# A four-layer graph network on one core: the test for the general path at the last head's end, layer 2's weights, degrees and first adjacency rows ahead of the skipped loops

## The chip, the cores and the metric

The kernel runs on one core of a Trainium2 chip. The metric is the device time of one execution in microseconds. The kernel before took 4518.02 us (median of three runs, 4509.77 to 4524.34).

## The reference

The input is a matrix x of N = 2708 nodes with C = 128 features and a weighted adjacency matrix adj (2708 x 2708, a few neighbours a row and the diagonal), all in float32. Four layers follow each other, each as x = x + layer(relu(layernorm(x))).

```python
# layer 0
d = adj.sum(1); s = 1 / (sqrt(d) + 1e-8)
out = (adj * s[:, None] * s[None, :]) @ (h @ W + b)
# layer 1: 128 "heads" d of width 8
q, k, v = (h @ Wq.T).reshape(128, n, 8), ...
a = softmax(q @ k.T * 128**-0.5 + adj + adj, axis=2)   # n x n for every head
out = (a @ v).reshape(n, 1024) @ Wo.T
# layer 2
deg = adj.sum(1, keepdims=True); deg = where(deg == 0, 1, deg)
t = (adj.T @ h / deg) @ W_n.T + b_n + h @ W_c.T + b_c
out = relu(gamma * (t - mean(t)) * rsqrt(var(t) + 1e-5) + beta)
# layer 3
gate[i, j] = sigmoid(a[j] + b[i] + b1) * adj[i, j]
out = einsum('ijf,jg->ig', gate, h) @ weight + bias
```

## The kernel before, in words

Nodes lie in 22 row tiles (NT = 22) of 128 partitions, the last of 20 rows (`rows`); x stays in SBUF as `x_sb`. Columns of a 2708-wide row are cut into six pieces of at most 512 (`cols`).

Layer 1 does not form its 128 softmax matrices. For every head the exponential is replaced by a polynomial in q·k, so that a head needs only features of its keys and queries (128 of each) and moments of its values; the adjacency bias acts only where adj is not zero, and is brought in as a correction, gathered neighbour by neighbour. One part of the program, `with tc.manual_schedule()`, is an order written out by hand. Its main loop runs over the heads (`for d in range(D)`, D = 128), and inside a head over six chunks of row tiles (`for c in range(NCH)`). A head's work:

- `keys` and `with_values` on POOL: features of the keys (`fk`) and values times features (`y`, L1010, 2 instructions a head).
- `queries` on DVE: features of the queries (`fq`, L1007).
- `moments` on PE (`m_ps`, L1048), then `weighted` on DVE (`mw`, L1058).
- `turn`: transposes of `fq` on PE (L1074) and their copy on ACT (L1076).
- `evaluate`: the product with the moments on PE (`g_ps`, L1086), and on DVE the multiplication `z` (L1094) and the reduction into `o_raw` (L1100).

Four heads make a group (GRP = 4), 32 groups in all. After a group `sums` adds the values' sum on POOL (L693) and SP stores it to `o_g` (L696).

Beside the heads run two things. `first` is a generator: the search for the neighbours and their gathers, logits and values, the corrections of the softmax (DMA_INDIRECT from POOL at L825, DVE at L840, L870, L878). PACE says how many of its steps are taken for each chunk; in the kernel before it is 1.30. Once `first` is exhausted, up to three calls of `step` a chunk work on the list `beside`: 32 `normalise(g)` and 22 `project_out(t)`. At most two of them are under way at a time, and each waits three chunks (WAIT) behind its loads. After the loop over the heads a `while` loop takes what is left in `beside`: I call this the drain.

- `normalise(g)` loads a group's sums and corrections (`r_raw` L921, `r_more` L922, on SP), adds them on DVE (L930), takes the reciprocal of the last column (L932), multiplies (`r_on`, L933), and stores the result to `o_c` in DRAM with 11 to 13 DMAs from SP (L399).
- `project_out(t)` loads the row tile of all heads (`o_cr`, L499), runs 16 matmuls on PE (L505) and four additions into `x_sb` on DVE (L508).

The polynomial holds only for small logits. So behind the drain the kernel before tests the bounds (L1183 to L1223, some 20 small DVE instructions and a few PE transposes), loads the answer into registers of all engines (`values_load`, L1226 and L1227), and has a general path of three hardware loops, `For_i(0, once)` at L1229, `For_i(0, heads)` at L1241 and `For_i(0, once)` at L1295. With these inputs the counts are zero and the loops are skipped; their barriers are not.

Layer 2 follows: weights by `transposed` (load L180, PE L186, copy on DVE L189), biases by `column_of` (L172), `norm_relu` (statistics on DVE L200 and L201, the square root on ACT L203, h on DVE L206 and ACT L210, transposes L217), the inverse degree `di` (L1323 to L1325) and its spread over all partitions `diB`: for each row tile `dg` on DVE (L1329), `d_ps` on PE (L1331), a copy on ACT (L1332). Then for each of the 22 row tiles one adjacency row block `a2` is loaded (L1339, four buffers), and six matmuls add into `pg` (L1341); `ag = pg * diB` (L1346), and the rest of layer 2 and layer 3 follow.

The tile framework places everything outside the hand-written order: each engine executes its own instruction queue, and DMAs are issued mostly by SP, in the order in which they stand there. An instruction that waits for a semaphore holds what stands behind it on its engine. At a hardware loop every engine waits for the others, and the loop's block waits for the DMAs that have been issued.

Of the kernel before, what the change touches and what calls it, by code (L numbers as in the profile page):

```python
# [9 lines left out]
FP = mybir.dt.float32  # L10
AF = mybir.ActivationFunctionType
# [5 lines left out]
P = 128  # L17
# [32 lines left out]
def gnn4_kernel(  # L50
# [75 lines left out]
    few = keep.tile([P, 1], FP, name="few")  # L126

# [388 lines left out]
    with ExitStack() as ph:  # L516
# [481 lines left out]
        PACE = 1.30  # L998
# [107 lines left out]
        with tc.manual_schedule():  # L1106
# [19 lines left out]
            for d in range(D):  # L1126
# [35 lines left out]
                if (d + 2) % GRP == 0 and (d + 2) // GRP + 1 < NG:  # L1162
                    soon.append(prepare((d + 2) // GRP + 1, got))
            while beside or under_way:
                if not step(n, NG):
                    n += 1


    with ExitStack() as ph:
        gp = ph.enter_context(tc.tile_pool(name="l1g", bufs=1))  # L1170
        gw = ph.enter_context(tc.tile_pool(name="l1g_w", bufs=2))
        g_l = ph.enter_context(tc.tile_pool(name="l1g_l", bufs=1, space=PSUM))
        g_t = ph.enter_context(tc.tile_pool(name="l1g_t", bufs=1, space=PSUM))
        g_o = ph.enter_context(tc.tile_pool(name="l1g_o", bufs=1, space=PSUM))
        q_f = dram.tile([N, P, HEAD], FP, name="q_f")
        k_f = dram.tile([N, P, HEAD], FP, name="k_f")
        v_f = dram.tile([N, P, VW], FP, name="v_f")
        o_f = dram.tile([N, P, HEAD], FP, name="o_f")

        nc.vector.memset(top, 0.0)  # L1183
        p2 = gp.tile([C, 2], FP, name="p2")
        for e in range(2):
            pt = g_t.tile([P, BK], FP, name="g_tr", tag="tr")
            nc.tensor.transpose(pt[:C, :P], most2[:, e], ident)
            nc.vector.tensor_reduce(p2[:, e : e + 1], pt[:C, :P], axis=AX.X, op=ALU.max)
        nc.vector.tensor_tensor(top[:, 0:1], p2[:, 0:1], p2[:, 1:2], ALU.mult)
        nc.vector.tensor_tensor(top[:, 1:2], p2[:, 0:1], p2[:, 1:2], ALU.max)  # L1190
        nc.vector.tensor_reduce(top[:, 2:3], nval, axis=AX.XY, op=ALU.max)
        nc.vector.tensor_reduce(top[:, 3:4], nval, axis=AX.XY, op=ALU.min)
        low = gp.tile([P, 1], FP, name="low")
        nc.vector.tensor_reduce(low, least, axis=AX.X, op=ALU.min)
        nc.vector.tensor_tensor(top[:, 3:4], top[:, 3:4], low, ALU.min)
        nc.vector.tensor_scalar_mul(top[:, 3:4], top[:, 3:4], -1.0)
        nc.vector.tensor_reduce(low, below, axis=AX.X, op=ALU.max)
        nc.vector.tensor_tensor(top[:, 3:4], top[:, 3:4], low, ALU.max)
        nc.vector.tensor_tensor(top[:, 3:4], top[:, 3:4], full, ALU.max)
        pt = g_t.tile([P, BK], FP, name="g_tr", tag="tr")  # L1200
        nc.tensor.transpose(pt[:4, :P], top, ident)
        t4 = gp.tile([4, 1], FP, name="top4")
        nc.vector.tensor_reduce(t4, pt[:4, :P], axis=AX.X, op=ALU.max)
        pt = g_t.tile([P, BK], FP, name="g_tr", tag="tr")
        nc.tensor.transpose(pt[:1, :4], t4, ident[:4, :4])
        bnd = gp.tile([1, 6], FP, name="bound")
        nc.vector.tensor_copy(bnd[:, :4], pt[:1, :4])
        nc.vector.tensor_scalar(
            bnd[:, 4:5], bnd[:, 0:1], MAX_LOGIT**2, None, ALU.is_le
        )  # L1210
        nc.vector.tensor_scalar(bnd[:, 2:3], bnd[:, 2:3], float(MAX_ADJ), None, ALU.is_le)
        nc.vector.tensor_tensor(bnd[:, 4:5], bnd[:, 4:5], bnd[:, 2:3], ALU.mult)
        nc.vector.tensor_scalar(bnd[:, 1:2], bnd[:, 1:2], MOST**2, None, ALU.is_le)
        nc.vector.tensor_tensor(bnd[:, 4:5], bnd[:, 4:5], bnd[:, 1:2], ALU.mult)
        nc.vector.tensor_scalar(bnd[:, 5:6], bnd[:, 3:4], 0.0, None, ALU.is_le)
        nc.vector.tensor_scalar(ovf, bnd[:, 5:6], -1.0, 1.0, ALU.mult, ALU.add)
        pt = g_t.tile([P, BK], FP, name="g_tr", tag="tr")
        nc.tensor.matmul(pt[:, :1], ones[0:1], bnd[:, 5:6], start=True, stop=True)
        nc.vector.tensor_copy(few, pt[:, :1])
        nc.vector.tensor_tensor(bnd[:, 4:5], bnd[:, 4:5], bnd[:, 5:6], ALU.mult)  # L1220
        flag = gp.tile([1, 2], I32, name="flag")
        nc.vector.tensor_scalar(flag[:, 0:1], bnd[:, 4:5], -1.0, 1.0, ALU.mult, ALU.add)
        nc.vector.tensor_scalar(  # L1223
            flag[:, 1:2], bnd[:, 4:5], -float(C), float(C), ALU.mult, ALU.add
        )
        once = nc.values_load(flag[:, 0:1], min_val=0, max_val=1)  # L1226
        heads = nc.values_load(flag[:, 1:2], min_val=0, max_val=C)  # L1227

        with tc.For_i(0, once):  # L1229
            for r0, sz in rows:  # L1230
                for at, dst in ((0, q_f), (HEAD, k_f), (2 * HEAD, v_f)):
                    b = gw.tile([P, P, dst.shape[2]], FP, name="bounce", tag="b")
                    nc.sync.dma_start(
                        b[:, :sz], qkv_c[:, r0 : r0 + sz, at : at + dst.shape[2]]
                    )
                    nc.sync.dma_start(dst[r0 : r0 + sz].rearrange("r c h -> c r h"), b[:, :sz])

        def flat(src):
            return src.rearrange("r c h -> (r c) h")

        with tc.For_i(0, heads) as d:  # L1241
            nat = []
            for src in (q_f, k_f, v_f):
                a = gp.tile([P, NT, src.shape[2]], FP, name=f"g_nat{len(nat)}")
                f = flat(src)[bass.ds(d * N, N)]
                load_rows(nc.sync, a, f)
                nat.append(a)
            q, k, v = nat
            kT = gp.tile([HEAD, N], FP, name="g_kT")
            for t, (r0, sz) in enumerate(rows):  # L1250
                pt = g_t.tile([P, BK], FP, name="g_tr", tag="tr")
                nc.tensor.transpose(pt[:HEAD, :sz], k[:sz, t], ident[:sz, :sz])
                nc.vector.tensor_copy(kT[:, r0 : r0 + sz], pt[:HEAD, :sz])
            o = gp.tile([P, NT, HEAD], FP, name="g_o")
            for t, (r0, sz) in enumerate(rows):
                an = gw.tile([P, N], FP, name="g_adj")
                nc.sync.dma_start(an[:sz], adj[r0 : r0 + sz])
                pt = g_t.tile([P, BK], FP, name="g_tr", tag="tr")
                nc.tensor.transpose(pt[:HEAD, :sz], q[:sz, t], ident[:sz, :sz])
                qT = gw.tile([HEAD, P], FP, name="g_qT")  # L1260
                nc.vector.tensor_copy(qT[:, :sz], pt[:HEAD, :sz])
                pl = g_l.tile([P, NC, BK], FP, name="g_l")
                for c, (c0, cw) in enumerate(cols):
                    nc.tensor.matmul(
                        pl[:sz, c, :cw], qT[:, :sz], kT[:, c0 : c0 + cw], start=True, stop=True
                    )
                    nc.vector.scalar_tensor_tensor(
                        an[:sz, c0 : c0 + cw],
                        pl[:sz, c, :cw],
                        0.5,  # L1270
                        an[:sz, c0 : c0 + cw],
                        ALU.mult,
                        ALU.add,
                    )
                mx = gw.tile([P, 1], FP, name="g_mx")
                nc.vector.tensor_reduce(mx[:sz], an[:sz], axis=AX.X, op=ALU.max)
                nc.vector.tensor_scalar_mul(mx[:sz], mx[:sz], -2.0)
                nc.scalar.activation(an[:sz], an[:sz], AF.Exp, bias=mx[:sz], scale=2.0)
                po = g_o.tile([P, VW], FP, name="g_acc")
                for m, (m0, mz) in enumerate(rows):  # L1280
                    pt = g_t.tile([P, BK], FP, name="g_tr", tag="tr")
                    nc.tensor.transpose(
                        pt[:mz, :sz], an[:sz, m0 : m0 + mz], ident[:sz, :sz]
                    )
                    pT = gw.tile([P, P], FP, name="g_pT")
                    nc.vector.tensor_copy(pT[:mz, :sz], pt[:mz, :sz])
                    nc.tensor.matmul(
                        po[:sz], pT[:mz, :sz], v[:mz, m], start=m == 0, stop=m == NT - 1
                    )
# [5 lines left out]
        with tc.For_i(0, once):  # L1295
# [6 lines left out]
            for t in range(NT):  # L1302
                for _ in project_out(gw, g_t, woT, t):
                    pass
# [297 lines left out]
```

## Time and profile before

| what | value |
|---|---|
| median of 3 runs | 4518.02 us (4509.77 to 4524.34) |
| profiled execution | 4486.52 us |
| its span | 4484.7 us |
| mean granted TensorE clock | 0.837 |
| busy: PE, DVE, ACT, POOL | 72%, 82%, 25%, 57% of the span |
| last reduction of the head loop ends | 3931.8 us |
| last addition of the drain ends | 4018.42 us |
| test ends | 4023.07 us |
| third skipped loop is left | 4032.78 us |
| first pg matmul | 4047.38 us |
| pg stage ends | 4156.75 us |

Times in the profile count from the span's start, in one execution on the chip. An instruction's row gives its start, its duration, the engine, the line of the kernel, the operation, the tiles that it writes and reads, and in brackets the idle time of its engine ahead of it with the instruction that ended it. The engines are PE (matrix products; PEld is its weight load), DVE (vector), ACT (scalar), POOL (GpSimd), and SP, which issues DMAs. The granted clock is the share of full speed that PE had.

### The profile page before, as it was taken

Reading aid. Unit: us, or ns where it says so; the run is one execution under the profiler, and the core shown is the slowest. Engines: PE = TensorE matmul, PEld = TensorE weight load, DVE = VectorE, ACT = ScalarE, POOL = GpSimd, SP = SyncE. Lnnn points to the kernel's source line nnn. Section 1 sums busy time; section 2 is a strip of 40 time slices with the busy share of each in tenths; the row PEclk is TensorE's granted clock in tenths of the full one; section 3 lists DMA queues with packets and bytes.
Section 4 is the critical chain, followed back from the end, with each engine's and each line's share of the span. In section 5 each row is a group of like instructions: output and inputs, shape, how many; then the busy total and the mean of one; then the engine's idle time right before and its main releaser. Section 6 shows DMA issues by size and latency. Waiting matters only on the chain. (4 is left out here: it accounts for less than half of the span.)

```text
span 4484.7 us, 49573 instructions
## 1 busy us (share of the span) xinstructions
PE 3225.3 (72%) x17298; PEld 2876.7 (64%) x17298; DVE 3669.4 (82%) x4983; ACT 1100.2 (25%) x2497; POOL 2544.8 (57%) x2253
## 2 busy tenths in 40 slices
PE   7985778889966677677777676667676687839634
PEld 5952777788856666667666676667666677824323
DVE  5988889998868999999999998999899888831323
ACT  4255233334412222222222222222122111101201
POOL 0001766678858666677676676767576555300076
PEclk9987888999988888888888888888888788959555
DMA  4647334357702222222222222222222344447132
GB/s 186 227 154 294 86 101 110 87 126 171 164 9 84 79 75 76 89 81 83 87 76 88 77 92 78 85 86 94 86 88 88 76 97 95 107 108 262 51 100 79
DMA packets 402005, 480.24 MB, mean 107 GB/s; under 512 B 290672, under 2 KB 322098, under 8 KB 376916
## 3 DMA queue, kind: packets, MB, share of 16 engines
q1 hardware_dynamic: 370140, 308.03, 23.8%
q0 software_dynamic: 31600, 168.86, 11.2%
q8 instruction: 144, 2.36, 0.2%
q14 instruction: 121, 0.99, 0.1%
HBM read 363.13 MB, written 113.67 MB: 106 GB/s over the span
## 5 line engine op out<-in xcount | busy, mean ns | idle before, releaser
L1086 PE MATMUL g_ps<-mw,fT 128*128 128x189 f32 x5632 | 1213.3, 362 | 734.6 <-DVE mw L1058 501.9
L1086 PEld LDWEIGHTS g_ps<-mw,fT 128*128 128x128 f32 x5632 | 1032.8, 213 | 812.8 <-issue 642.2
L1010 POOL TENSOR_TENSOR y<-bk,raw 128x2079 f32<-128x2079 f32 x256 | 982.9, 3840 | 685.7 <-PE m_ps L1048 658.4
L1048 PE MATMUL m_ps<-y,fk 128*128 128x189 f32 (+1 forms) x5632 | 1108.1, 342 | 29.0 <-POOL y L1010 29.0
L1048 PEld LDWEIGHTS m_ps<-y,fk 128*128 128x128 f32 (+1 forms) x5632 | 969.2, 204 | 58.1 <-POOL y L1010 29.5
L1076 ACT COPY fT<-f_ps 128x512 f32<-128x512 f32 (+1 forms) x768 | 422.9, 551 | 1955.2 <-PE f_ps L1074 1954.3
L1094 DVE TENSOR_TENSOR z<-g_ps,bq 128x756 f32<-128x756 f32 (+1 forms) x768 | 669.1, 871 | 177.7 <-PE g_ps L1086 173.9
L1100 DVE TENSOR_REDUCE o_raw<-z 128x36 f32<-128x756 f32 (+1 forms) x768 | 672.5, 876 | 26.3
L1010 POOL TENSOR_TENSOR fk<-bk,raw 128x528 f32<-128x528 f32 (+1 forms) x512 | 526.5, 1058 | 0.0
L1074 PE MATMUL f_ps<-ident,fq 128*128 128x128 f32 x2816 | 490.8, 299 | 46.2 <-DVE fq L1007 44.6
L1074 PEld LDWEIGHTS f_ps<-ident,fq 128*128 128x128 f32 x2816 | 399.2, 157 | 83.9 <-issue 45.8
L1010 POOL TENSOR_TENSOR fk<-raw,bk 128x352 f32<-128x352 f32 (+1 forms) x512 | 337.3, 688 | 0.0
L840 DVE TENSOR_TENSOR c_z<-c_kv,c_q 128x1024 f32<-128x1024 f32 (+1 forms) x121 | 308.1, 2546 | 5.3 <-DMA c_kv<-kv_n,srt 5.3
L1007 DVE TENSOR_TENSOR fq<-bq,q_ps 128x528 f32<-128x528 f32 (+1 forms) x512 | 288.1, 605 | 0.0
L825 POOL DMA_INDIRECT c_kv<-kv_n,srt x121 | 139.1, 1150 | 244.3 <-DVE c_v L870 142.4
L1010 POOL TENSOR_TENSOR bk<-raw 128x88 f32<-128x88 f32 (+1 forms) x512 | 238.3, 496 | 34.6 <-DMA raw<-qkv_c 34.1
L878 DVE TENSOR_TENSOR c_acc<-c_acc,c_v 128x1152 f32<-128x1152 f32 (+1 forms) x99 | 248.2, 2507 | 2.5
L465 POOL MEMSET qkv<- 128x512 f32 x6 | 6.3, 1076 | 373.7 <-PE l_o L350 254.3
L870 DVE TENSOR_TENSOR c_v<-c_kv,c_c 128x1024 f32<-128x1024 f32 (+1 forms) x99 | 205.9, 2080 | 0.0
L1420 POOL DMA_INDIRECT g<-gate_d,srt x121 | 122.0, 1008 | 107.9 <-issue 105.1
L505 PE MATMUL l_o<-woT,o_cr 128*128 128x128 f32 (+1 forms) x352 | 94.8, 425 | 107.6 <-DMA o_cr<-o_c 68.6
L1007 DVE TENSOR_TENSOR fq<-q_ps,bq 128x352 f32<-128x352 f32 (+1 forms) x512 | 171.7, 378 | 0.0
(284 smaller groups left out, 3490.2 us busy)
## 6 DMA issues: line engine op xcount, KB each, us to landing
a_nat<-in_adj_dram SPq DMA_DIRECT2D x32, 1354.0 KB
qkv_c<-qkv SPq DMA_DIRECT2D x5, 6400.0 KB
a<-in_adj_dram SPq DMA_DIRECT2D x21, 1354.0 KB
kv_n<-n_kv SPq DMA_DIRECT2D x32, 672.0 KB
an<-in_adj_dram SPq DMA_DIRECT2D x15, 1354.0 KB
o_g<-o_raw SPq DMA_DIRECT2D x32, 396.0 KB
r_raw<-o_g SPq DMA_DIRECT2D x32, 396.0 KB
r_more<-more_n SPq DMA_DIRECT2D x32, 396.0 KB
```

The lines of the kernel that those rows point to most:

```text
L825: nc.gpsimd.indirect_dma_start(out=kvs[b][:sz, e].rearrange("p c e k -> p (c e k)"), out_offset=None, in_=kv_n.rearrange("n c k -> n (c k) ...
L840: nc.vector.tensor_tensor(z[:sz], kvs[b][:sz, e, :, 0], qs[t][:sz], ALU.mult)
L870: nc.vector.tensor_tensor(z[:sz, :, :HEAD], kv[:sz, e, :, 1], c[:sz, e, :, None].to_broadcast([sz, C, HEAD]), ALU.mult,)
L878: nc.vector.tensor_tensor(acc[:sz], acc[:sz], z[:sz], ALU.add)
L1007: nc.vector.tensor_tensor(o, x, y, ALU.mult)
L1010: nc.gpsimd.tensor_tensor(o, x, y, ALU.mult)
L1048: nc.tensor.matmul(pms[d][:, : B_ALL * VW], fks[d][:sz, t], ys[d, h][:sz, m].rearrange("p k b -> p (k b)"), start=t == 0, stop=t == NT - 1,)
L1074: nc.tensor.transpose(pt[:, m], fqs[d][:, t0 + m], ident)
L1076: nc.scalar.copy(fts[d, c][:, :n], pt[:, :n])
L1086: nc.tensor.matmul(pg[:, m, : B_ALL * VW], ft[:, m], mws[d].rearrange("p k b -> p (k b)"), start=True, stop=True,)
L1094: nc.vector.tensor_tensor(z[:, :n], pg[:, :n, : B_ALL * VW].rearrange("p t (k b) -> p t k b", k=VW), bqs[d % 2][:, t0 : t0 + n, None, :B_A ...
L1100: nc.vector.reduce_sum(ros[g][:, t0 : t0 + n, i], z[:, :n], axis=AX.X,)
```

## The change

Four things change.

1. PACE goes from 1.30 to 1.38.
2. The test of the bounds moves from behind the drain to the end of the loop over the heads, ahead of the drain in the program's text, and into the hand-written order's block; its small tiles come from layer 1's pools, and `flag` from the pool that stays.
3. Layer 2's pools are opened ahead of the general path. The weights, the biases, `di`, `diB` (with PSUM buffers of their own, `l2_ps0`) and the loads of the first four adjacency row blocks are written ahead of `values_load` and the loops.
4. The general path itself is unchanged, now nested in layer 2's block. `norm_relu` and the pg loop follow it; the pg loop takes the loaded blocks from the list `natural`.

```diff
-        PACE = 1.30
+        PACE = 1.38
...
+            nc.vector.memset(top, 0.0)
+            p2 = sm.tile([C, 2], FP, name="p2")
...
+            nc.vector.tensor_scalar(flag[:, 0:1], bnd[:, 4:5], -1.0, 1.0, ALU.mult, ALU.add)
+            nc.vector.tensor_scalar(
+                flag[:, 1:2], bnd[:, 4:5], -float(C), float(C), ALU.mult, ALU.add
+            )
+
             while beside or under_way:
                 if not step(n, NG):
                     n += 1
...
-        nc.vector.memset(top, 0.0)
...
-        once = nc.values_load(flag[:, 0:1], min_val=0, max_val=1)
-        heads = nc.values_load(flag[:, 1:2], min_val=0, max_val=C)
...
     with ExitStack() as ph:
         lp = ph.enter_context(tc.tile_pool(name="l2", bufs=1))
         wk_pool = ph.enter_context(tc.tile_pool(name="l2w", bufs=2))
         ap = ph.enter_context(tc.tile_pool(name="l2_adj", bufs=4))
+        natural = []
+
+        def rows_of_adj2(t):
+            r0, sz = rows[t]
+            a = ap.tile([P, N], FP, name="a2")
+            nc.sync.dma_start(a[:sz], adj[r0 : r0 + sz])
+            natural.append(a)
+
+        with tc.tile_pool(name="l2_ps0", bufs=2, space=PSUM) as ps:
+            wnT = transposed(lp, wk_pool, ps, wn2, "wnT")
+            wcT = transposed(lp, wk_pool, ps, wc2, "wcT")
+            bias = column_of(lp, bn2, "bn2_sb")
...
+            diB = lp.tile([P, N], FP, name="diB")
+            for t, (r0, sz) in enumerate(rows):
+                dg = lp.tile([P, P], FP, name="dg", tag="dg", bufs=2)
+                nc.vector.tensor_scalar_mul(dg[:sz, :sz], ident[:sz, :sz], di[:sz, t : t + 1])
+                pd = ps.tile([P, BK], FP, name="d_ps", tag="tr")
+                nc.tensor.matmul(pd[:, :sz], ones[:sz], dg[:sz, :sz], start=True, stop=True)
+                nc.scalar.copy(diB[:, r0 : r0 + sz], pd[:, :sz])
+        for t in range(min(4, NT)):
+            rows_of_adj2(t)
+
+        with ExitStack() as gh:
...
+            once = nc.values_load(flag[:, 0:1], min_val=0, max_val=1)
+            heads = nc.values_load(flag[:, 1:2], min_val=0, max_val=C)
+
+            with tc.For_i(0, once):
...
         ps = ph.enter_context(tc.tile_pool(name="l2_ps", bufs=2, space=PSUM))
-        wnT = transposed(lp, wk_pool, ps, wn2, "wnT")
...
         h, hT = norm_relu(lp, ps, "2")
...
             for t, (r0, sz) in enumerate(rows):
-                a = ap.tile([P, N], FP, name="a2")
-                nc.sync.dma_start(a[:sz], adj[r0 : r0 + sz])
+                if t >= len(natural):
+                    rows_of_adj2(t)
+                a = natural[t]
```

## The prediction

> **What bounds the kernel now.** The change touches the stretch from the end of layer 1's head loop to layer 2's first large product, so I read the span in windows first (columns: window; its length; busy us and instructions of PE, PEld, DVE, ACT, POOL; granted clock; DMA share; GB/s).
>
> ```profile
> 1000.00:1100.00 100.00, 94.70 (x600) 88.85 (x599) 82.97 (x141) 42.45 (x86) 83.59 (x76) 1.00 0.72 168
> 3700.00:3800.00 100.00, 73.88 (x393) 70.50 (x392) 82.89 (x116) 15.40 (x35) 50.48 (x43) 0.85 0.41 95
> 3900.00:4000.00 100.00, 42.56 (x186) 39.03 (x184) 44.28 (x73) 3.78 (x7) 2.52 (x1) 0.64 0.58 134
> 4080.00:4090.00 10.00, 10.00 (x28) 4.73 (x27) 0.00 (x0) 0.00 (x0) 0.00 (x0) 1.00 0.84 290
> ```
>
> Heads alone are bound by PE (row 1); heads with normalisations keep DVE 83% busy (row 2); in row 3 nothing is busy: the loop has ended and the last normalisations and projections run as a chain. Row 4 is layer 2's adjacency product: PE is full and nothing else matters. The timeline gives the chain its marks (start, us, instruction, idle before and its releaser):
>
> ```profile
> 3931.06 0.74 DVE L1100 TENSOR_REDUCE o_raw<-z 128x27 f32<-128x567 f32 x1
> 3986.69 0.98 DVE L930 TENSOR_TENSOR r_raw<-r_raw,r_more 128x792 f32<-128x792 f32 x1 [4.58 <-DMA r_more<-more_n]
> 4022.94 0.13 DVE L1223 TENSOR_SCALAR flag<-bound 1x1 int32<-1x1 f32 x1
> 4032.78 0.13 POOL L197 MEMSET mv<- 128x44 f32 x1 [98.38 <-PEq L1295]
> 4038.65 0.29 DVE L189 COPY wnT<-w_ps 128x128 f32<-128x128 f32 x1 [2.80 <-PE w_ps L186]
> 4042.86 1.28 ACT L203 ACT_TABLE_LOAD   x1 [113.96 <-DVE mv L201]
> 4156.86 3.30 DVE L1346 TENSOR_TENSOR ag<-pg,diB 128x512 f32<-128x512 f32 x6 [88.22 <-PE pg L1341]
> ```
>
> The head loop ends at T0 = 3931.8. Then come the drain (7 normalisations, 7 projections; its last x_sb add starts at 4018.14 and ends at 4018.42) 86.6 us; the test 4.65; two register loads and three skipped loops 9.7 (4023.07 to 4032.78); layer 2 up to the first pg matmul at 4047.38, 14.6; the pg stage to 4156.75, 109.4. From T0 that is 224.95 us. All of it is on the path, and behind it both kernels are alike.
>
> **The change part by part.** The instruction order of the changed kernel settles three things that its text does not. PACE 1.38 exhausts the corrections near head 106 instead of 113, so 5 normalisations and 3 projections go from the drain into the head loop. The first register load and the first skipped loop stand not behind the drain but in its middle, with 2 normalisations and 4 projections left. And on SP the biases' loads wait for the last projection's PE, so nothing of layer 2 runs beside those normalisations: the 22 dg→d_ps→diB steps run alone after them, then come the other two loops, and only adjacency rows 0 and 1 are issued ahead of them.
>
> *Head loop, longer by X.* Normalisations among the heads have rows of their own (groups by line, 3526 to 3932; columns: busy us, mean ns):
>
> ```profile
> L933 DVE TENSOR_TENSOR r_on<-r_raw,r_rs 128x704 f32<-128x704 f32 x25 | 52.4, 2096 | 4.7 <-DMA o_c<-r_on 3.9
> L930 DVE TENSOR_TENSOR r_raw<-r_raw,r_more 128x792 f32<-128x792 f32 x26 | 38.2, 1468 | 2.8 <-DMA r_more<-more_n 2.8
> L932 DVE RECIPROCAL r_rs<-r_raw 128x88 f32<-128x88 f32 x25 | 17.6, 702 | 0.8
> L508 DVE TENSOR_TENSOR x_sb<-x_sb,l_o 128x128 f32<-128x128 f32 x60 | 17.1, 285 | 25.7 <-PE l_o L505 23.9
> ```
>
> By DVE time: 5×(2.10+1.47+0.70) + 3×4×0.285 = 25 us. By difference: heads 18 to 35, with no side work, start 18.0 us apart; the last 14.2 heads took 406 us, 150 over 18.0 each, for 25 normalisations and 15 projections, 6.0 us a normalisation with its 0.6 of a projection: 5×6.0 = 30. Seven heads also change sides. They leave a stretch where DVE is 94 to 98% busy, freeing 7×14.9/0.96 = 109 us (14.9 is 83% of 18.0), and join one where a head costs 18.0: 126, so +17; but they bring 7×3.1 = 22 us of idle DVE, in which side work fits. I take 0 for this, and X = 30, nearest to the row by difference. Bounds: 12 (operations free of POOL: 5×2.7+3×1.1 = 17, less 5) and 61 (rival one).
>
> *First part of the drain and loop 1.* Before, from T0 to the second-last normalisation at 3986.69: 54.9 us; this goes, with five normalisations and three projections. In its place POOL's sum of the last group (L693, 2.52 us from 3931.88), the store and three loads issued behind it on SP (some 1.6 us), their landing (r_more 3981.28 to 3986.69 and others, 4 to 5 us) and the loop's exit, 1.6: 10.5 us. The loop's block waits for every DMA issued. The test's 4.65 us of short DVE and PE instructions lies beside those loads; without that cover it would cost 4.65. The loop's barrier holds all engines; what is queued behind it is the next normalisation, which waits for those loads anyway.
>
> *Rest of the drain.* 2 normalisations and 4 projections: 3986.69 to 4018.42, unchanged, 31.7.
>
> *Weights, degrees alone.* Their weight loads were issued long before and are free. In the pg stage these 22 steps cost PE little: a d_ps pair with one 0.857 us pg matmul cycles in 1.30 us, so 0.44 a pair, 4.9 in all. Alone each is a chain, dg 0.25 (DVE), d_ps about 0.27 (PE), diB 0.27 (ACT), with two buffers. The nearest row is layer 2's y_tr→x_sb pairs at 4173 to 4183, 0.44 us each with one hop less; I take 0.6: 13 us and a lead of 2, 15 (bounds 9.5 and 18).
>
> *Loops 2 and 3.* Layer 3's two loops with two loads took 7.46 (4247.45 to 4254.91); the three loops here 9.71, so 2.25 a loop and 1.48 a load: 2×2.25+1.48 = 6.0. Rows 0 and 1 have landed by then (rows are 1354 KB, some 4.5 us each at about 300 GB/s), hidden beside the diB chain. Bounds 6 and 10, the latter if they have not.
>
> *Layer 2's start.* The wait of 2.80 for w_ps, the two weight copies, the bias add, the three instructions of L1323 to L1325 and the first two of L1329 leave this stretch: 14.6 becomes 9.7. The table load (1.28 us) no longer sits behind the statistics. *pg stage:* 109.4 − 4.9 = 104.5. Advance rows bring it nothing: PE is 10.00 of 10 us busy, and
>
> ```profile
> SPq L1339 <- PE pg L1341: 86.4, 18, 10.7
> ```
>
> shows the loads waiting for PE to free buffers, not the reverse.
>
> Sum from T0: 10.5+31.7+15+6.0+9.7+104.5 = 177.4, against 224.95: −47.5. With X = +30: −17.5. The profiled execution took 4486.52 us (span 4484.7), 0.7% under the median of 4518.02; I carry the difference over as it is: 4501.
>
> **A rule against it.** The loop's price hangs on POOL's long y (3.78 us each):
>
> ```profile
> 3814.25 3.77 POOL L1010 TENSOR_TENSOR y<-bk,raw 128x2079 f32<-128x2079 f32 x1
> 3814.36 4.41 DVE L933 TENSOR_TENSOR r_on<-r_raw,r_rs 128x704 f32<-128x704 f32 x1
> ```
>
> L933 takes 0.89 in the drain, where POOL is still, and 4.41 here: it ends with y. The Trainium skill, "SBUF — State Buffer", section "Who interferes with whom", says that a VectorE instruction with two SBUF inputs contends with a GpSimd one that reads SBUF, and that whichever starts first holds the port for its whole length. By that rule every L930 and L933 that starts behind a y pays its remainder, in the head loop alone; were all ten to, the sum would be +28 over mine by DVE time.
>
> **The rivals.**
> *One, slower: the five normalisations meet y.* Place: L930 and L933 in the head loop. The longest of them in 3526 to 3932 took 4.56 and 4.52. If all five normalisations pay that, 5×(4.56+0.70+4.52) = 49, and three projections at PE's 67.3/15 = 4.5 add 12 as PE holds the next head: X = 61, net +13, 4531. It decides from X = 47.5, 9.5 us a normalisation. For: z and fq queue behind each held operation. Against: the mean rows, 2.1 and 1.5, are a third of that.
> *Two, much faster: side work fills idle DVE.* X = 12: −35, 4483. For: DVE is 17% idle in row 2. Against: 406 us for 14.2 heads had the same idle time and did not absorb it.
> *Three, no gain: what is taken from the drain comes back as waits.* Loop 1 waits for slow landings (+4), the chain at the cold clock takes 18 (+3), rows 0 and 1 hold loop 2 (+4), X = 35 (+5): net −1.5, 4516. For: the title's "beside" does not happen, as the order shows; each piece stands alone at a low clock (0.64 in row 3).
>
> **How the numbers follow.** My forecast has 0.45 (own range 4488 to 4512), rival one 0.20, two 0.16, three 0.19. A run of this kernel can tell about 0.3%, 13.5 us, from no change. Faster by more: 0.36 of the forecast's 0.45 and all of two, 0.52. Within: 0.09 and 0.17 of three, 0.26. Slower: one and 0.02 of three, 0.22. The range runs from below two (X = 12 with the chain at 9.5: −40.5, 4477, and a few us for heads absorbing more) to one: 4474 to 4533.
>
> **What would show it.** Right: corrections end near head 106; the head loop's last reduce some 30 us later; a skipped loop about 10 us after it; a lone diB chain of some 15 us; first pg about 73 us after the loop's last reduce instead of 115.6; pg stage 104 to 105. Wrong: the loop longer by more than 47, L930 and L933 means near 4 us, a diB chain beyond 20, or skipped loops that take over 5 us each; or a drain with more than two normalisations behind loop 1.

## The result, and the profile after

The changed kernel took 4503.9 us (median of six runs, 4493.72 to 4514.37), the kernel before 4521.18 beside it: ratio 0.9958, 95% interval 0.9937 to 0.9979, so 19 us less (9 to 28). The forecast was 17 less.

The two profiled executions must not be subtracted from each other. That of before (4486.52) lies 35 us under its kernel's median, that of after (4514.37, span 4512.6) 10 over; the last section says where some of this lies. Stretches can be compared. The windows of the kernel after, columns as before:

```profile
1000.00:1100.00 100.00, 94.41 (x598) 88.55 (x597) 83.44 (x140) 42.18 (x86) 81.77 (x73) 1.00 0.79 186
3700.00:3800.00 100.00, 73.43 (x400) 69.91 (x401) 79.46 (x117) 14.73 (x37) 50.92 (x43) 0.85 0.44 95
3900.00:4000.00 100.00, 81.80 (x494) 76.02 (x493) 78.22 (x144) 18.12 (x41) 45.86 (x37) 0.94 0.17 42
4090.00:4100.00 10.00, 10.00 (x29) 4.85 (x28) 0.00 (x0) 0.00 (x0) 0.00 (x0) 1.00 0.85 309
```

Heads alone, heads with normalisations and the pg stage look as they did. The third row, mostly the drain before, now holds heads up to 3988: the loop ends later and its last heads have no side work, so PE is busy at a high clock. The chain's marks in the timeline:

```profile
3987.31 0.74 DVE L1101 TENSOR_REDUCE o_raw<-z 128x27 f32<-128x567 f32 x1
3998.75 0.98 DVE L931 TENSOR_TENSOR r_raw<-r_raw,r_more 128x792 f32<-128x792 f32 x1 [3.57 <-SPq L1266]
4032.91 0.28 DVE L509 TENSOR_TENSOR x_sb<-x_sb,l_o 20x128 f32<-20x128 f32 x1 [0.16 <-PE l_o L506]
4044.51 0.50 ACT L1247 COPY diB<-d_ps 128x128 f32<-128x128 f32 x2 [0.41 <-PE d_ps L1246]
4051.39 0.49 DVE L201 BATCH_NORM_STATS2 ln_st<-x_sb 128x6 f32<-128x128 f32 x2 [7.32 <-PEq L1332]
4060.75 3.75 PE L1353 MATMUL pg<-a,h 128*128 128x512 f32 x6
4165.83 3.30 DVE L1358 TENSOR_TENSOR ag<-pg,diB 128x512 f32<-128x512 f32 x6 [97.35 <-PE pg L1353]
```

Counted from T0, the end of the loop's last reduction (3988.05 here, 3931.80 before): the first skipped loop releases DVE after 10.7 us (row 2; its releaser is the loop's line); the drain's last addition ends 34.4 later; the lone degrees take 11.8 (to the end of row 4), the last two loops 6.4 (row 5), layer 2's start 9.4, the pg stage 105.1. Together 177.8 us against 225.1 before: 47.3 us less behind the head loop. A total that falls by 19 therefore means a head loop that is longer by 28, plus or minus the interval's 10, since what follows the pg stage is the same code in both kernels.

The normalisations among the heads (groups by line, 3430 to 3988) and the wait for adjacency buffers on SP:

```profile
L934 DVE TENSOR_TENSOR r_on<-r_raw,r_rs 128x704 f32<-128x704 f32 x30 | 58.5, 1950 | 7.5 <-DMA o_c<-r_on 6.7
L931 DVE TENSOR_TENSOR r_raw<-r_raw,r_more 128x792 f32<-128x792 f32 x30 | 47.2, 1574 | 3.1 <-DMA r_more<-more_n 3.1
L933 DVE RECIPROCAL r_rs<-r_raw 128x88 f32<-128x88 f32 x30 | 21.1, 703 | 1.0
L509 DVE TENSOR_TENSOR x_sb<-x_sb,l_o 128x128 f32<-128x128 f32 x72 | 20.5, 285 | 32.2 <-PE l_o L506 30.5
```

```profile
SPq L1225 <- PE pg L1353: 87.0, 18, 16.6
```

Thirty normalisations are in the loop now, as foretold, and one costs DVE 4.23 us (4.27 before). SP still waits 87 us for PE in the pg stage: the rows loaded early bring it nothing.

### The profile page after: what moved, and what is told of

The parts are those of the page before. It is cut to its first block, busy times and chain, and to the rows that moved or that the text cites. A ratio compares the mean times of both kernels' runs of the same rounds, so it can differ in the third digit from the quotient of the medians.

```text
span 4512.6 us, 49502 instructions
## 1 busy us (share of the span) xinstructions
PE 3240.9 (72%) x17298; PEld 2893.1 (64%) x17298; DVE 3691.5 (82%) x4983; ACT 1100.5 (24%) x2497; POOL 2543.6 (56%) x2253
## 5 line engine op out<-in xcount | busy, mean ns | idle before, releaser
L841 DVE TENSOR_TENSOR c_z<-c_kv,c_q 128x1024 f32<-128x1024 f32 (+1 forms) x121 | 292.3, 2416 | 0.0
L879 DVE TENSOR_TENSOR c_acc<-c_acc,c_v 128x1152 f32<-128x1152 f32 (+1 forms) x99 | 269.0, 2717 | 3.1 <-DVE c_v L871 0.5
```

Source lines behind the costliest of these rows:

```text
L841: nc.vector.tensor_tensor(z[:sz], kvs[b][:sz, e, :, 0], qs[t][:sz], ALU.mult)
L879: nc.vector.tensor_tensor(acc[:sz], acc[:sz], z[:sz], ALU.add)
```

## The experiments

Theory one, that of the prediction: the pace carries the gain, by moving five normalisations and three projections from the drain into the head loop, which pays about 30 us. Theory two: the moved test and layer 2's early set-up carry it, and the pace only shifts work. "Behind" is the distance from the last reduction to the pg stage's end, from the profile (before: 225.1); it differed by less than 1 us between two executions of one kernel (171.5 and 172.3, 160.9 and 161.6, below). The loop's own change is what is left of the total. Each ratio is to the kernel before on the same chip.

**One part alone: the pace.**

```diff
-        PACE = 1.30
+        PACE = 1.38
```
(on the kernel before)

> The kernel before with PACE 1.38 and nothing else. Theory one (the pace carries the gain): five normalisations and three projections leave the drain, whose 86.6 us become about 41; the test (4.65), the three loops (9.7), layer 2's start (14.6) and the pg stage (109.4) stay, so the head loop's last reduce stands about 179 us ahead of the pg stage's end instead of 225, -46; the head loop pays about 30; net -16 us, ratio 0.9965. Theory two (the moved test and the early set-up carry it, the pace only shifts work): what leaves the drain is paid in full in the head loop, net 0, ratio 1.000 within 0.002.

Ratio 0.9966 (0.9946 to 0.9987), -15 us (6 to 24 less); behind 179.6:

```profile
3984.22 0.74 DVE L1100 TENSOR_REDUCE o_raw<-z 128x27 f32<-128x567 f32 x1
4164.58 3.30 DVE L1346 TENSOR_TENSOR ag<-pg,diB 128x512 f32<-128x512 f32 x6 [88.22 <-PE pg L1341]
```

The pace alone gives the forecast -45 behind the loop, and +30 in it (21 to 40): nearly the whole change.

**All but the pace.**

```diff
-        PACE = 1.38
+        PACE = 1.30
```
(on the changed kernel)

> The changed kernel with PACE back at 1.30. Theory one: seven normalisations stay behind the head loop, so the drain is as long as before with one loop's barrier inside it; test hidden (-4.65), two loops behind instead of three (-3), layer 2's start 9.4 instead of 14.6 (-5), pg stage 105 instead of 109.4 (-4.4), a lone diB chain (+11.8): from the last reduce to the pg stage's end about 220 instead of 225, the loop unchanged, net -5 us, ratio 0.999. Theory two: -17 us, ratio 0.996.

Ratio 1.0003 (0.9987 to 1.0020); behind 225.0:

```profile
3932.70 0.74 DVE L1101 TENSOR_REDUCE o_raw<-z 128x27 f32<-128x567 f32 x1
4158.41 3.30 DVE L1358 TENSOR_TENSOR ag<-pg,diB 128x512 f32<-128x512 f32 x6 [97.11 <-PE pg L1353]
```

Behind the loop the rest of the change is worth nothing, where I had expected -5 (the total's interval alone would still allow -5). Four terms cancel. The drain's last addition ends 90.1 us behind T0 instead of 86.6, with the loop's barrier inside it: +3.5. From there to layer 2's first statistics it takes 20.4 us instead of 15.1, since the lone degrees cost more than the test and one loop give back: +5.3. Layer 2's start is 4.7 and the pg stage 4.1 shorter. Theory two, which had the gain here, is refuted.

**Degrees and rows back behind the loops.** The block `di` to `diB` stands after `norm_relu` again, and the advance loads go:

```diff
-        for t in range(min(4, NT)):
-            rows_of_adj2(t)
...
         h, hT = norm_relu(lp, ps, "2")
+        di = lp.tile([P, NT], FP, name="di")
...
+            nc.scalar.copy(diB[:, r0 : r0 + sz], pd[:, :sz])
```

> The changed kernel with the degrees (di, diB) and the first adjacency rows behind the loops again, as in the kernel before; pace, test and weights as changed. Theory one: the lone diB chain of 11.8 us is gone, of which some 3 remain as the landing of the biases' loads ahead of the second loop; the pg stage is longer by 4 to 5; rows issued after the loops land within the 9.4 us of layer 2's start. From the last reduce to the pg stage's end about 174 us, against 177.7 in the changed kernel: so these two parts of the change cost a little. Theory two (they gain): 185 or more, with first pg waiting for its row by 3 us or more.

One execution, not timed. Behind 171.5, 6.2 us less than in the changed kernel:

```profile
4122.12 3.30 DVE L1356 TENSOR_TENSOR ag<-pg,diB 128x512 f32<-128x512 f32 x6 [89.25 <-PE pg L1351]
```

(T0 is 3950.58 here.) So writing degrees and rows ahead of the loops costs 6: the lone chain takes 11.8 us and gives back 4.1 in the pg stage and 1.6 in the two loops. The rows, which were moved in the same edit, give nothing to speak of: the first pg matmul comes 9.6 us after the first statistics here and 9.4 with early rows. This execution's head loop was also 34 and 37 us shorter than in the pace alone's and the changed kernel's profiles, so the kernel was timed:

> The kernel of the third experiment again (degrees and first rows behind the loops, the rest as changed), timed, because its one execution had a head loop some 35 us shorter than the changed kernel's with the same instructions in it. If that was one execution's luck: the distance from the last reduce to the pg stage's end is 171 to 172 us, 6 less than in the changed kernel, and the time is 53 less behind the loop and 30 more in it than before, -23 us, ratio 0.995. If the arrangement really shortens the head loop: ratio 0.990 or lower.

Ratio 0.9917 (0.9886 to 0.9948), -37 us, behind 172.3: the head loop pays 15 by the total, with an interval of 1 to 29. The ratio lies between the two that I had named; its interval holds the 0.990 of one and ends just under the 0.995 of the other, so the run does not decide between them, and the short loop is not shown to belong to the kernel: 1 to 29 overlaps the changed kernel's 19 to 38. The 6 us behind are shown, in two executions.

**The test alone moved**, PACE 1.30, layer 2 as before:

```diff
+            nc.vector.memset(top, 0.0)
...
             while beside or under_way:
```
(the block of the test, from behind the drain to here)

> The kernel before with the test alone at the head loop's end; PACE 1.30, layer 2 as before. Theory one: the test's 4.65 us disappear beside the drain's loads, the first loop's barrier falls into the drain and costs at most its exit, the other two stay behind it: from the last reduce to the pg stage's end 216 to 222 us instead of 225. Theory two: the barrier in the drain breaks its overlap and the gain of the test is lost: 225 or more.

One execution, not timed. Behind 219.5, 5.6 less than before:

```profile
3940.62 0.74 DVE L1101 TENSOR_REDUCE o_raw<-z 128x27 f32<-128x567 f32 x1
4030.13 0.28 DVE L509 TENSOR_TENSOR x_sb<-x_sb,l_o 20x128 f32<-20x128 f32 x1 [2.11 <-SPq L1242]
4160.83 3.30 DVE L1347 TENSOR_TENSOR ag<-pg,diB 128x512 f32<-128x512 f32 x6 [88.84 <-PE pg L1342]
```

The first loop stands ahead of the drain's last addition here (DVE leaves it at 4030.0 us; row 2 names SP, which is at the second loop by then), and the drain is 2.4 longer; the test and one loop are gone from behind it, 7.3 us from the drain to the statistics instead of 15.1. With the second experiment this closes the account: the test's move gives 5.6, the early set-up takes 5.5 (6.2 for degrees and rows at 1.38), and together they leave the 225.0 above.

**One loop, degrees by a DMA, rows at the pg stage.**

```diff
+    di_d = dram.tile([NT, P], FP, name="di_d")
...
+        nc.tensor.transpose(pd[:NT, :P], di, ident)
+        nc.vector.tensor_copy(dT, pd[:NT, :P])
+        nc.sync.dma_start(di_d, dT)
...
+        nc.sync.dma_start(
+            diB, di_d.rearrange("t p -> (t p)")[:N].partition_broadcast(P)
+        )
...
             with tc.For_i(0, once):
...
-            with tc.For_i(0, heads) as d:
+                with tc.For_i(0, heads) as d:
```

> The changed kernel with the three skipped loops nested in one, so that one barrier is left (in the drain), the inverse degrees transposed and written to DRAM ahead of layer 1 and read back to all partitions by one DMA beside the pg stage, and the adjacency rows loaded at the pg stage. Theory one: from the last reduce to the pg stage's end 45 for the drain with its loop, 10 for layer 2's start, 105 for pg: 160 us instead of 177.7; with the loop's +30 the time is -35 us against before, ratio 0.992. Rival: what the loops and the diB chain took was cover for loads, and layer 2's first rows are late now: 168 or more, ratio 0.994 or higher.

Ratio 0.9906 (0.9871 to 0.9941), -42 us, behind 160.9: theory one's number, but not at its places.

```profile
3978.49 0.74 DVE L1114 TENSOR_REDUCE o_raw<-z 128x27 f32<-128x567 f32 x1
4019.12 0.28 DVE L509 TENSOR_TENSOR x_sb<-x_sb,l_o 20x128 f32<-20x128 f32 x1 [0.17 <-PE l_o L506]
4025.65 0.49 DVE L201 BATCH_NORM_STATS2 ln_st<-x_sb 128x6 f32<-128x128 f32 x2 [5.19 <-issue]
4140.16 3.30 DVE L1363 TENSOR_TENSOR ag<-pg,diB 128x512 f32<-128x512 f32 x6 [97.47 <-PE pg L1358]
```

I had put the one loop into the drain, 45 us for both. It stands behind the drain: 40.2 for the drain, 6.2 from there to the statistics. Layer 2's start (9.4) and the pg stage (105.1) stay as they were, so what the other loops and the diB chain took covered nothing.

**The price of the pace inside the head loop.** All side work is taken out of the loop and left to the drain, with both paces:

```diff
-                        for _ in range(3):
-                            step(n, max(d // GRP - 1, 0))
+                        pass
```

> The kernel before without any normalisation or projection inside the head loop: all 32 and 22 run in the drain, PACE 1.30. The head loop shrinks by the side work's price, 25 normalisations with 15 projections at 6.0 us a normalisation: -150 us; the drain grows by 25 x about 12 us = 300. Ratio about 1.03. The pair of this run and the next splits the 30 us that the head loop pays for the pace.

> The same with PACE 1.38. Here the pace can only exchange heads beside corrections for heads alone. If the 30 us are the price of the five normalisations and three projections, as the prediction had it: the same time as with 1.30, within 8 us. If the exchange of heads costs (126 against 109 us, and nothing to fill the idle DVE): +17 us. If a denser pace hurts the corrections' stage itself: +25 or more.

1.0287 (1.0249 to 1.0324) and 1.0259 (1.0222 to 1.0296). With 1.30 the distance behind grows by 278 us (I expected 300) and so the head loop shrinks by 148 (150). I expected the second to equal the first within 8 us; its median is 16 lower, with intervals that overlap. The last correction and the loop's last reduction, before, changed, and in these two:

```profile
3524.01 4.31 DVE L878 TENSOR_TENSOR c_acc<-c_acc,c_v 20x1152 f32<-20x1152 f32 x1
3428.70 1.35 DVE L879 TENSOR_TENSOR c_acc<-c_acc,c_v 20x1152 f32<-20x1152 f32 x1 [0.46 <-DVE c_v L871]
3549.08 4.38 DVE L878 TENSOR_TENSOR c_acc<-c_acc,c_v 20x1152 f32<-20x1152 f32 x1
3804.83 0.74 DVE L1100 TENSOR_REDUCE o_raw<-z 128x27 f32<-128x567 f32 x1
3414.29 1.35 DVE L878 TENSOR_TENSOR c_acc<-c_acc,c_v 20x1152 f32<-20x1152 f32 x1
3784.62 0.74 DVE L1100 TENSOR_REDUCE o_raw<-z 128x27 f32<-128x567 f32 x1
```

In the profiles of the two the corrections end at 3553.5 and 3415.6 us, with 14.17 and 20.67 heads to go (counted by the z instructions behind them), and these take 252.1 and 369.7 us: 17.8 and 17.9 a head, PE's pace without side work. With 17.95 a head (most of these last heads start 17.94 apart) the same count gives the price of the side work in the other kernels:

| kernel | heads left | stretch, us | over 17.95 a head | normalisations in it | each |
|---|---|---|---|---|---|
| before | 14.17 | 403.5 | 149.2 | 25 | 6.0 |
| all but the pace | 14.17 | 403.5 | 149.2 | 25 | 6.0 |
| changed | 20.67 | 558.0 | 187.0 | 30 | 6.2 |
| pace alone | 20.67 | 551.5 | 180.6 | 30 | 6.0 |

The stretch grows by 148 to 155 us: 6.5 heads x 17.95 = 117, and 31 to 38 for the five normalisations and three projections. Against this the corrections end earlier. In the four profiles with side work, PACE 1.38 and layer 2 as changed or before (changed, pace alone, the two with degrees and rows back) they end at 3400 to 3433; in the three with 1.30 (before, all but the pace, test alone) at 3528 to 3538; the means are 3420 and 3532, 112 us apart, and 138 in the pair above. So the exchange of heads is between +5 and -21 us, and what it is in one execution varies more than that. The totals say much the same: +30 less 31 for the pace alone, +28 less 38 for the changed kernel, -17 for the pair.

**Other paces**, on the one-loop version:

```diff
-        PACE = 1.38
+        PACE = 1.34
```
(and 1.46, 1.60)

> The one-loop version with the degrees spread by a DMA, PACE 1.34 instead of 1.38. The corrections end some 3.5 heads later, and 2 to 3 normalisations more stay for the drain or for the last heads. If pace only pays by filling the head loop (theory one), heads without side work at the end are waste and 1.34 loses nothing: the same as 1.38 within 8 us. If heads alone are cheaper than heads beside corrections (the pair without side work: -16 us for 0.08), it is slower by about 8, and by what stays for the drain, some 13 a normalisation.

> The same version with PACE 1.38, repeated beside the other paces on one chip: ratio 0.990 to 0.992 against the kernel before.

> The same version with PACE 1.46: the corrections end near head 100, about 12 heads at the end have no side work. Nothing more can leave the drain, since the last two groups end with the last heads. Theory one with the exchange at zero: the same as 1.38 within 6 us. If the exchange gains 16 us for 0.08: 0.0035 lower than 1.38. If a denser pace hurts: 0.003 or more higher.

> The same version with PACE 1.60. With the exchange at zero: as 1.38. If it gains 16 us for each 0.08: 0.0095 lower than 1.38, ratio about 0.982. If a denser pace hurts the corrections' stage: higher than 1.38 by 0.005 or more.

| PACE | ratio to before | 95% interval | behind, us | head loop against before, us |
|---|---|---|---|---|
| 1.34 | 0.9906 | 0.9881 to 0.9932 | 160.8 | +22 |
| 1.38 | 0.9920 | 0.9896 to 0.9944 | 161.6 | +27 |
| 1.46 | 0.9975 | 0.9957 to 0.9992 | 162.3 | +51 |
| 1.60 | 0.9923 | 0.9901 to 0.9945 | 160.9 | +30 |

Behind the loop all are equal: with 1.34 already only two normalisations are left, so my 13 us a normalisation were not due. In the loop 1.46 costs 24 us more than 1.38, and 1.60 does not. None of the three rules I had written down fits both: exchange at zero fits 1.60, a denser pace that hurts fits 1.46, and -16 for each 0.08 fits neither. In the two profiles, whose loops differ by 27, 12 lie in the exchange (5.8 more heads alone cost 105, the corrections' earlier end frees 93) and 15 in the stretch with the normalisations (195.4 us over 17.95 a head, against 180.1). Why 1.46 is worse stays open. The version with 1.34 is below both kernels in time, 0.9906 against the changed kernel's 0.9958; that it is better than the same version with 1.38 is not shown.

## Why the prediction was right

- *Behind the loop.* Foretold 177.4, measured 177.8, and the places were right. By terms: first skipped loop 10.5, 10.7; rest of the drain 31.7, 34.4 (SP comes out of the loop's barrier and its register loads last and issues the first store 2.4 us after `r_on` is done, where it took 0.03 before; I had counted this at nothing); lone diB chain 15, 11.8 (about 0.5 us a step; the granted clock was 1.00 in the windows from 4034 to 4044, not low as rival three had it); last two loops 6.0, 6.4; layer 2's start 9.7, 9.4; pg 104.5, 105.1. Two misses of 3 cancel, which is luck: the sum is nearer than its terms.
- *In the loop.* X = +30 foretold, +28 (19 to 38) from the changed kernel's total and +30 (21 to 40) from the pace alone. The price by difference, 6.0 us a normalisation with its part of a projection, is what four profiles show. DVE's own time explains 4.2 of it, and 0.7 more with the additions of 0.6 of a projection; what makes up the last 1.1 was not traced.
- *The exchange at zero* was a choice, and it stands only within about 20 us. My bound of 109 freed against 126 paid was too dear: 6.5 heads changed sides, not seven, and 112 to 138 are freed against 117.
- *What carries the gain.* The sum put nearly all of it on the pace, though it did not say so in a line: 54.9 us of drain removed, against 10.5 that come in their place. The experiments show it: the pace alone -15, the rest 0.
- *Rival one* (the normalisations meet POOL's y) did not decide: L931 and L934 average 1.57 and 1.95, not 4.5. The Trainium skill's rule ("SBUF — State Buffer", "Who interferes with whom"), that a VectorE instruction with two SBUF inputs contends with a GpSimd one that reads SBUF, agrees with the rows that last 4 us. But only 14 of the 60 in the changed kernel's loop last over 3 us: against the lone rows of 0.98 and 0.89 it is 1.65 us a normalisation on average, not 7.
- *Rival two* needed X = 12; the changed kernel's and the pace's intervals begin at 19 and 21. *Rival three* had the right places: the barrier did cost the drain 3, and the early set-up took 6. But it also needed a chain of 18 us, a head loop longer by 35 and late rows, and these did not come.
- *What the prediction read or added wrongly.* Heads 18 to 35 start 19.2 us apart on average, not 18.0; with 19.2 the price by difference would have given X = 27. That 18.0 was near the truth is luck: the kernels without side work show 17.8 and 17.9. The heads that changed sides left a stretch with DVE 91% busy (3300 to 3528), not 94 to 98. The row of 4.41 us does not end with y but 0.75 us behind it, so it waits for y and then runs, which is what the rule would have it do. In rival one three projections at 4.5 add 13.5, not 12, and the means 2.1 and 1.5 are a half and a third of its 4.5. The mark "first pg" of before is the weight load, 0.26 us ahead of the matmul, which shifts that much between two terms and leaves the sum. None of this moves the forecast by more than 3 us.

## What to carry to other kernels

Look at where a scheduler puts an instruction before you credit a move: here "ahead of the skipped loops" meant alone behind the last projection, and the moved set-up took what the moved test earned. Price side work in a loop by the loop's own stretches with and without it, not by the busy time of its instructions. When two profiled executions differ by more than the change, compare distances between marks inside each, and take the rest from the medians.

## What had not been expected of the hardware

The stretch from the pg stage's end to the last instruction is the same code in all kernels. It took 327 to 330 us in nine profiled executions and 346 to 350 in five, one kernel showing both: with degrees and rows back 327.4 the first time and 345.9 the second. In windows of 25 us of that stretch POOL, which issues the gathers there, fell from about 19 us busy to 14 to 17 in the longer ones. The record names the chip of twelve of these executions, and it separates them: all four on one chip (the second run of degrees and rows back, the first of the one loop, the two without side work) are long, all eight on two others short. The kernel before, timed on the same three chips, had a median of 4521 us on the first and of 4493 and 4492 on the others. Each chip was used in one session, so whether the chip or the session decides was not tried; that it is not the single execution is what the twelve say.

The chip of the first two profiles is not on record, but that of before has a short stretch (327.9) and that of after a long one (346.7). So 19 us of the 28 between them lie behind the pg stage, in code that the change does not touch, and the prediction's difference between profile and median (31.5 us) has the size of the difference between the chips (28 to 29).

The time of the heads beside corrections differs by some 30 us between executions with the same instructions, while the stretch of heads with normalisations behind it repeats to 0.1 us in three kernels with 1.30 (403.5) and within 7 with 1.38 (550.8 to 558.0).
